# Pairwise outer products with batch norm: where the output runs of the long rows are cut

## The chip, the cores and the metric

The kernel runs on one core of a Trainium2 chip. The metric is the device time of one execution in microseconds (us). Four runs of the kernel before gave 1876.79 to 1878.18 us, with a median of 1877.02 us.

## The reference, cut to what matters

Two inputs `xi` and `xj` have the shape (1024 samples, 39 features, 16). For each of the 741 feature pairs (r, c) with c < r and each sample, the 16 x 16 outer product of `xj[r]` and `xi[c]` is taken, normalised per pair over all samples, and multiplied by a 16 x 16 weight:

```python
rows, cols = np.tril_indices(39, k=-1)                       # 741 pairs
cross  = xj[:, rows, :, None] * xi[:, cols, None, :]         # 1024 x 741 x 16 x 16
mean   = cross.mean((0, 2, 3));  var = ((cross - mean) ** 2).mean((0, 2, 3))
normed = (cross - mean) * rsqrt(var + 1e-5) * gamma + beta
out    = normed * W                                          # 776.99 MB of f32
```

The inputs are 6 MB; the output is 777 MB. "Row r" below means the r pairs (r, 0) to (r, r-1), which lie side by side in the output: r KB (r times 256 f32) of each sample.

## The kernel before, in words

The 1024 samples lie on 128 partitions with 8 samples each. The statistics come first, in about the first 40 us; they give a scale and a shift for every pair. The rest of the time is a stream of **tiles**. A tile is one row r of T = 2 samples (t = 0 and 1) on all partitions. The list `tiles` (lines 67 to 76) starts with the four tiles of row 19 (n = 0 to 3), then goes through row 20 with row 18, row 38 alone, row 37 with row 1, row 36 with row 2, and so on to row 21 with row 17, four sample pairs for each. From row 37 on, a long row and its partner row 38 - r fill together one half, a **slot**, of the buffer `y_sb`; the two slots are used in turn (`slot ^= 1`). So while one slot leaves for memory, the other is computed, and a slot can be overwritten only when its stores have landed.

For each tile the engines do this:

- `scale_xi` (line 163): GpSimd (POOL) multiplies `xi` by the scale, two tiles ahead.
- `products` (line 177): for t = 0 and then t = 1, 16 products, one for each i; ScalarE (ACT, line 147) does the first 11 or 12 of them and POOL (line 149) the rest. Each product writes all pairs of one sample. So the products of sample t wait until all earlier runs of that sample in the slot have landed.
- `finish` (line 256): the shift and the weight. VectorE (DVE) does a pair of both samples in one `scalar_tensor_tensor` (line 293), in the order of the pairs; POOL does a few pairs. In a row above `LONG` = 33 these are eight pairs before the middle (pairs 10 to 17 of row 37): ACT adds the shift (line 277) and POOL multiplies four pairs at a time (line 282). In a row up to 33 these are the last pairs (28 to 31 of row 32), shift and weight both on POOL (lines 279 and 282).
- `store` (line 205): SyncE (SP) issues the transfer of a piece of a row when its pairs are ready. All stores are issued on SP, in order, and share one queue into the core's 16 DMA engines (q1 of the profile).

`bounds` (line 247) cuts a row into pieces, and `store` into runs. A tile with n >= 8 and a row up to `WHOLE` is stored by sample: the pieces of t = 0 each by a run of its own, and t = 1 by one run of the whole row at the end. A row above `WHOLE` sends the first piece of both samples as one run, and then the last piece of each sample. A row up to `ONE` has a single piece:

| row | runs before: pair range and sample |
|---|---|
| 38 | 0:19 both; 19:38 t0; 19:38 t1 |
| 37 | 0:18 both; 18:37 t0; 18:37 t1 |
| 36 | 0:19 t0; 19:36 t0; 0:36 t1 |
| 35, 34, 33 | 0:20, 0:21, 0:22 of t0; the rest of t0; all of t1 |
| 32 | 0:23 t0; 23:32 t0; 0:32 t1 |
| 31 | 0:24 t0; 24:31 t0; 0:31 t1 |
| 30 to 20 | all of t0; all of t1 |

Rows below 19 send one run of both samples. The program order (line 525) is, for each n: `scale_xi(n + 2)`, `finish(n)`, `products(n + 1)`. The loop `for n in range(1, len(tiles))` has four long tiles to each row; with their partners between them the tiles of row 37 are n = 16, 18, 20, 22, those of row 32 are n = 56, 58, 60, 62, and those of row 31 are n = 64, 66, 68, 70. The tile that used a slot before tile n is tile n - 4 of the same kind (n = 14 for n = 16, whose row 38 has no partner, and so on).

Of the kernel before, what the change touches and what calls it, by code (L numbers as in the profile page):

```python
# [15 lines left out]

ONE, LONG, WHOLE = 30, 33, 36
FIRST_PIECES = (  # L20
    (0, 1, 3, 6, 10, 14, 19), (0, 4, 9, 14, 19), (0, 4, 11, 19), (0, 9, 19), (0, 10, 20), (0, 9, 18), (0, 10, 20), (0, 9, 18)
)
# [541 lines left out]
```

## Time and profile before

| | |
|---|---|
| median of four runs | 1877.02 us |
| the profiled execution: its time | 1878.18 us |
| the profiled execution: span from first to last instruction | 1876.5 us |
| DVE, ACT, POOL busy | 1723.7, 1645.3, 1535.5 us (92, 88, 82% of the span) |
| written to HBM | 776.99 MB, 417 GB/s over the span |
| DMA packets of the store queue (q1) | 53344, busy 98.0% of 16 engines' span |
| chain of waits: DMA, ACT, DVE | 54%, 21%, 19% of the span |

In the profile DVE, ACT, POOL and SP are the engines, a "q" behind a name means the engine's instruction sequencer (SPq issues DMAs), and L216 is line 216 of the kernel. A row of a timeline gives the start, the duration, the engine, the line, the operation, what it writes and reads, and in brackets the idle time before it and what ended that idle time. A row of DMA issues gives how many were issued in the window asked for, the KB of each, and the time from issue to landing. With the issue time from the timeline, issue plus this time is when the data has landed.

### The profile page before, as it was taken

The page shows a single profiled execution, that of the slowest core. Times are in us where ns is not written, and L with a number is a line of the kernel's source. Part 1 is how long each engine was busy: PE and PEld are TensorE (multiplying, and loading weights), DVE is VectorE, ACT ScalarE, POOL GpSimd, SP SyncE. Part 2 cuts the span into 40 slices and gives each one's busy share as a digit, 9 for nine tenths or more (in the row PEclk, how much of TensorE's full clock was granted, in tenths as well). Part 3 has the DMA queues.
Part 4 walks back from the last instruction along what each step waited for, and adds up shares of the span by engine and source line. Part 5 has one row for each costly group of instructions (what it writes and reads, how often), then busy time and mean ns, then how long its engine had stood idle before and what let it go on. Part 6 is the DMA issues. An engine that isn't in the chain of part 4 may idle for free.

```text
span 1876.5 us, 9638 instructions
## 1 busy us (share of the span) xinstructions
PE 26.0 (1%) x130; PEld 23.3 (1%) x130; DVE 1723.7 (92%) x2640; ACT 1645.3 (88%) x3416; POOL 1535.5 (82%) x1746
## 2 busy tenths in 40 slices
PE   4000000000000000000000000000000000000000
PEld 4000000000000000000000000000000000000000
DVE  8999888899999999999999999999999999999994
ACT  7999888898888899989999999998999998989892
POOL 8999877787777788888888888888888888888882
DMA  5999999999999999999999999999999999999998
GB/s 191 386 422 419 431 424 425 426 425 425 425 425 428 428 426 426 425 426 425 423 426 425 433 424 427 429 425 431 424 431 426 429 425 429 429 425 431 428 425 350
DMA packets 54714, 783.63 MB, mean 418 GB/s; under 512 B 4720, under 2 KB 6384, under 8 KB 17520
## 3 DMA queue, kind: packets, MB, share of 16 engines
q1 hardware_dynamic: 53344, 779.72, 98.0%
q10 hardware_dynamic: 1296, 3.29, 0.5%
q14 instruction: 73, 0.60, 0.1%
q8 instruction: 1, 0.02, 0.0%
HBM read 6.00 MB, written 776.99 MB: 417 GB/s over the span
## 4 chain that ended last, share of the span: by engine, by line
DMA 54%; ACT 21%; DVE 19%; issue 3%; POOL 2%; SPq 0%; ACTq 0%; DVEq 0%; PE 0%; POOLq 0%
DMA out_dram<-y_sb 54%; ACT y_sb L147 20%; DVE y_sb L293 18%; POOL y_sb L149 1%; DVE y_sb L360 1%; POOL y_sb L282 0%; ACT y_sb L230 0%; DVE y_sb L334 0%; POOL xs L169 0%; DMA xi_sb<-in_r_xi_dram 0%; POOL y_sb L279 0%; SPq L216 0%; POOL y_sb L344 0%; ACT y_sb L277 0%; DVE y_sb L192 0%
## 5 line engine op out<-in xcount | busy, mean ns | idle before, releaser
L293 DVE SCALAR_TENSOR_TENSOR y_sb<-y_sb,st_sb,w_dve 128x512 f32<-128x512 f32 (+1 forms) x2511 | 1653.1, 737 | 115.5 <-issue 101.6
L147 ACT ACTIVATE y_sb<-xs,xj_sb 128x288 f32<-128x288 f32 (+20 forms) x3194 | 1513.8, 565 | 179.8 <-DMA out_dram<-y_sb 147.3
L149 POOL TENSOR_SCALAR y_sb<-xs,xj_sb 128x480 f32<-128x480 f32 (+27 forms) x1126 | 606.9, 566 | 8.5 <-DMA out_dram<-y_sb 8.4
L282 POOL TENSOR_TENSOR y_sb<-y_sb,w_sb 128x2048 f32<-128x2048 f32 (+3 forms) x155 | 517.8, 3346 | 89.8 <-ACT y_sb L277 80.2
L169 POOL TENSOR_TENSOR xs<-xi_sb,st_sb 128x640 f32<-128x640 f32 (+33 forms) x135 | 184.3, 1365 | 198.2 <-ACT y_sb L147 194.4
L279 POOL TENSOR_SCALAR y_sb<-y_sb,st_sb 128x512 f32<-128x512 f32 x291 | 197.6, 696 | 5.1 <-ACT y_sb L147 5.1
L277 ACT ACTIVATE y_sb<-y_sb,st_sb 128x512 f32<-128x512 f32 x160 | 100.2, 708 | 4.0 <-POOL y_sb L149 2.3
L192 DVE TENSOR_TENSOR y_sb<-xs,ps 128x256 f32<-128x256 f32 (+3 forms) x32 | 24.8, 817 | 0.6
L491 PE MATMUL ps<-y_sb 39*128 39x38 f32 (+37 forms) x76 | 16.4, 397 | 2.8 <-DVE y_sb L477 2.8
L491 PEld LDWEIGHTS ps<-y_sb 39*128 39x128 f32 x76 | 16.3, 329 | 3.1 <-DVE y_sb L477 3.1
L355 ACT ACTIVATE y_sb<-y_sb 128x1248 f32<-128x1248 f32 x8 | 10.0, 1244 | 2.9 <-POOL y_sb L344 1.8
L344 POOL TENSOR_TENSOR y_sb<-xi_sb,y_sb 128x1248 f32<-128x1248 f32 x4 | 9.2, 2329 | 3.2 <-ACT y_sb L393 3.2
L360 DVE TENSOR_REDUCE y_sb<-y_sb 128x78 f32<-128x1248 f32 x8 | 11.2, 1446 | 0.4 <-ACT y_sb L355 0.4
L147 ACT ACTIVATE y_sb<-xi_sb,xj_sb 128x304 f32<-128x304 f32 x24 | 11.4, 537 | 0.0
L239 DVE TENSOR_TENSOR y_sb<-y_sb,w_dve 128x2048 f32<-128x2048 f32 (+4 forms) x6 | 10.7, 1837 | 0.1
L334 DVE TENSOR_REDUCE y_sb<-xi_sb 128x39 f32<-128x624 f32 (+1 forms) x6 | 6.1, 1013 | 3.9 <-DMA xi_sb<-in_r_xi_dram 3.9
L344 POOL TENSOR_TENSOR y_sb<-xj_sb,y_sb 128x1248 f32<-128x1248 f32 x4 | 9.2, 2330 | 0.0
L380 PE MATMUL ps<-y_sb 128*39 128x79 f32 x48 | 8.1, 340 | 16.2 <-DVE y_sb L360 16.0
L232 POOL TENSOR_SCALAR y_sb<-y_sb,st_sb 128x512 f32<-128x512 f32 x8 | 6.5, 816 | 2.1 <-ACT y_sb L147 2.1
L334 DVE TENSOR_REDUCE y_sb<-xj_sb 128x39 f32<-128x624 f32 (+1 forms) x6 | 6.1, 1015 | 0.8 <-DMA xj_sb<-in_r_xj_dram 0.8
L230 ACT ACTIVATE y_sb<-y_sb,st_sb 128x512 f32<-128x512 f32 x9 | 6.5, 803 | 0.2 <-ACT y_sb L147 0.2
L380 PEld LDWEIGHTS ps<-y_sb 128*39 128x39 f32 x48 | 5.8, 177 | 18.2 <-DVE y_sb L360 10.6
(59 smaller groups left out, 37.4 us busy)
## 6 DMA issues: line engine op xcount, KB each, us to landing
out_dram<-y_sb SPq DMA_DIRECT2D x16, 3072.0 KB, 21.9
out_dram<-y_sb SPq DMA_DIRECT2D x20, 2432.0 KB, 12.5
out_dram<-y_sb SPq DMA_DIRECT2D x10, 4608.0 KB, 15.1
out_dram<-y_sb SPq DMA_DIRECT2D x12, 3840.0 KB, 21.6
out_dram<-y_sb SPq DMA_DIRECT2D x16, 2816.0 KB, 22.4
out_dram<-y_sb SPq DMA_DIRECT2D x12, 3584.0 KB, 23.1
out_dram<-y_sb SPq DMA_DIRECT2D x12, 3328.0 KB, 24.4
out_dram<-y_sb SPq DMA_DIRECT2D x15, 2560.0 KB, 11.9
```

What stands on the lines that cost most here:

```text
L147: nc.scalar.activation(y, src, AF.Copy, scale=scale)
L149: engine.tensor_scalar(y, src, scale, 1.0, ALU.mult, ALU.mult)
L169: nc.gpsimd.tensor_tensor(xs, xi_sb[:, t0 : t0 + T, 0:r, :], s_sb[:, :, n0 : n0 + r, :].to_broadcast([P, T, r, E]), ALU.mult,)
L192: nc.vector.tensor_tensor(view(n)[:, t].rearrange("p n (i j) -> p n i j", j=E), xs[:, t].unsqueeze(2).to_broadcast([P, r, E, E]), xj_short ...
L277: nc.scalar.activation(y[:, :, c, :], y[:, :, c, :], AF.Identity, bias=t_c)
L279: nc.gpsimd.tensor_scalar(y[:, :, c, :], y[:, :, c, :], t_c, 1.0, ALU.add, ALU.mult)
L282: nc.gpsimd.tensor_tensor(y[:, :, c0:c1, :], y[:, :, c0:c1, :], w_sb.unsqueeze(1).to_broadcast([P, T, c1 - c0, EE]), ALU.mult,)
L293: stt(y[:, t : t + size, c, :], y[:, t : t + size, c, :], t_sb[:, n0 + c : n0 + c + 1], w_dve.to_broadcast([P, size, EE]), ALU.add, ALU.mult,)
L344: nc.gpsimd.tensor_tensor(devs[n % 7], sources[x][:, t0 : t0 + T], shift[:, x : x + 1, :].unsqueeze(3).to_broadcast([P, T, F, E]), ALU.sub ...
L360: nc.vector.tensor_reduce(to[:, t0 : t0 + T, F : 2 * F], devs[n % 7], AX.X, ALU.add)
L380: nc.tensor.matmul(ps_g[acc][0:F, 0 : 2 * F + 1], lhs, fb[:, t], start=t == 0, stop=t == NT - 1)
L491: nc.tensor.matmul(ps[:, :, first[r] - n0 : first[r] - n0 + r], pick[:, r, :], stq[:, :, 0:r], start=True, stop=True,)
```

## The change

Three limits are raised. Nothing else is edited.

```diff
-ONE, LONG, WHOLE = 30, 33, 36
+ONE, LONG, WHOLE = 32, 33, 37
```

`bounds` and `store` read them (lines 247 to 254 and 205 to 219), and these runs differ:

| row | runs before | runs after |
|---|---|---|
| 37 | 0:18 both; 18:37 t0; 18:37 t1 | 0:19 t0; 19:37 t0; 0:37 t1 |
| 36 | 0:19 t0; 19:36 t0; 0:36 t1 | 0:21 t0; 21:36 t0; 0:36 t1 |
| 35 | 0:20 t0; 20:35 t0; 0:35 t1 | 0:21 t0; 21:35 t0; 0:35 t1 |
| 34 | 0:21 t0; 21:34 t0; 0:34 t1 | 0:23 t0; 23:34 t0; 0:34 t1 |
| 33 | 0:22 t0; 22:33 t0; 0:33 t1 | 0:23 t0; 23:33 t0; 0:33 t1 |
| 32 | 0:23 t0; 23:32 t0; 0:32 t1 | 0:32 t0; 0:32 t1 |
| 31 | 0:24 t0; 24:31 t0; 0:31 t1 | 0:31 t0; 0:31 t1 |

The arithmetic, its order on DVE, ACT and POOL, and the order of the bytes by sample within rows 36 to 31 stay as they are. Eight transfers fewer are issued, one for each tile of rows 32 and 31.

## The prediction

> **What bounds the kernel now.** I read the page's slices first, then the chain of waits, then the single stores.
>
> ```profile
> DMA  5999999999999999999999999999999999999998
> GB/s 191 386 422 419 431 424 425 426 425 425 425 425 428 428 426 426 425 426 425 423 426 425 433 424 427 429 425 431 424 431 426 429 425 429 429 425 431 428 425 350
> q1 hardware_dynamic: 53344, 779.72, 98.0%
> ```
>
> The DMA engines are full from the second slice to the last, at about 426 GB/s whatever the row: the output's bytes set the time. A change in how runs are cut can win little here, but it can lose: a moment in which the queue is empty is added to the end. So the question is how much work the queue still holds when the next store comes. The chain of waits in rows 33 and 32:
>
> ```profile
> 727.62 18.88 DMA out_dram<-y_sb
> 746.50 0.02 issue
> ...
> 750.16 19.90 DMA out_dram<-y_sb
> 770.06 0.02 issue
> ```
>
> This is a loop: the landing of sample 1 (746.50, 770.06) frees a slot, ACT goes on, and later that slot's stores are issued. The timeline gives its length:
>
> ```profile
> 770.14 21.18 ACT L147 ACTIVATE y_sb<-xs,xj_sb 128x512 f32<-128x512 f32 x48 [2.38 <-DMA out_dram<-y_sb]
> 777.69 18.52 DVE L293 SCALAR_TENSOR_TENSOR y_sb<-y_sb,st_sb,w_dve 128x512 f32<-128x512 f32 x28 [1.75 <-issue]
> ```
>
> The first 12 of the 48 products (sample 1 of tile 60) end at 777.6, and DVE's 28 pairs at 0.66 us end at 796.21. SP issues then. From landing to the end of the row it is 796.28 - 770.06 = 26.22 us, in all four tiles of row 32. The stores themselves, issues from the timeline and KB with time to landing from the DMA issues, for row 5's last store and the second piece of row 32 (tile 56), and two stores early in the run:
>
> ```profile
> 729.90 0.38 SPq L216 DMA_DIRECT2D out_dram<-y_sb  x1
> 749.73 0.33 SPq L216 DMA_DIRECT2D out_dram<-y_sb  x1
> ...
> 61.68 0.33 SPq L216 DMA_DIRECT2D out_dram<-y_sb  x1
> 64.43 0.38 SPq L216 DMA_DIRECT2D out_dram<-y_sb  x1
> ```
>
> ```profile
> out_dram<-y_sb SPq DMA_DIRECT2D x1, 1280.0 KB, 19.7
> out_dram<-y_sb SPq DMA_DIRECT2D x1, 1152.0 KB, 9.8
> ...
> out_dram<-y_sb SPq DMA_DIRECT2D x1, 640.0 KB, 3.4
> out_dram<-y_sb SPq DMA_DIRECT2D x1, 1024.0 KB, 4.0
> ```
>
> I call the landing of the last store issued so far, less the time of the next issue, the **lead**. When row 32's first piece is issued, at 746.51, the queue holds work until 729.90 + 19.7 = 749.6, a lead of 3.1 us. No lead behind the start-up is under 1.4 us (row 38: 240.10 + 16.7 against an issue at 255.36). How much lead is needed shows at 64.43: the queue ended at 61.68 + 3.4 = 65.1 (lead 0.6); 1024 KB take 2.4 us (two stores of 2432 KB, issued at 214.76 and 215.14 and landing after 13.3 and 18.7 us, lie 5.7 us apart: 434 GB/s); but it landed at 68.4, 1.6 us after its issue and 2.4 more. The store at 68.92 found an empty queue and gives 1.6 us too. So a **dry spell** is 1.6 us less the lead, if that is positive.
>
> **The change part by part.** *Row 32.* DVE's order stays, so the single run of sample 0 goes out when now the second piece does, 3.2 us later than the first piece. The leads at that time, from the partner's last store (row 5 or 6) and the second piece's issue:
>
> - tile 56: 749.6 - 749.73 = -0.1, a dry spell of 1.7 us
> - tile 58: 753.09 + 20.6 - 772.72 = 1.0; plus 1.7
> - tile 60: 776.09 + 20.6 - 796.28 = 0.4
> - tile 62: 799.65 + 20.4 - 819.26 = 0.8
>
> Now the loop counts. The dry spell ahead of tile 56 delays the queue's end by 1.7, but tile 58 comes 26.22 us after tile 54's landing, which is not delayed: its lead is 2.7, no loss. Tile 60 comes after tile 56's landing, 1.7 later like the queue: lead 0.4 as before, dry for 1.2. Tile 62 has 0.8 + 1.2 = 2.0: none. Row 32 costs 1.7 + 1.2 = 2.9 us. Behind the waiting store SP holds only sample 1's store and the partner's; sample 1's is issued 0.4 us later in either case, and ACT waits for its landing, which moves with the queue.
>
> *Row 31.* The same sum with 7 KB partners: 822.63 + 21.3 - 841.67 = 2.3, then 1.7, 2.6 and 1.6 us. Nothing, but with no reserve. Row 30, which already leaves this way, has 3.2 us at 934.54.
>
> *Row 37.* The first run now carries one sample: 2432 KB or 5.7 us in place of 4608 KB, while the next store comes 7.5 us after it. When it is issued is set by POOL, not by DVE:
>
> ```profile
> 290.49 9.97 DVE L293 SCALAR_TENSOR_TENSOR y_sb<-y_sb,st_sb,w_dve 128x512 f32<-128x512 f32 x15 [3.36 <-ACT y_sb L147]
> 293.19 9.01 POOL L282 TENSOR_TENSOR y_sb<-y_sb,w_sb 128x2048 f32<-128x2048 f32 x2 [5.67 <-ACT y_sb L277]
> ```
>
> POOL ends at 302.20 and the store is issued at 302.24; DVE's eleventh pair (pair 18, the added one) is done at 290.49 + 11 x 0.66 = 297.8, so it costs nothing. Tile 16: the queue ends at 263.85 + 17.1 = 281.0, with the short run at 286.7; the second run comes at 285.50: lead 1.2, dry for 0.4. Tile 18: 287.21 + 17.2 + 0.4 + 5.7 = 310.5 against 309.70: 0.8, dry for 0.8. Tiles 20 and 22 gain: sample 0 now lands ahead of sample 1's bytes, some 5 us sooner, so ACT need not wait for it as it does for 3.25 us ahead of 321.17. For tile 20 ACT can begin when its shifts end, 295.5, and is through sample 0's 11 products at 303.0; sample 1's landing, 285.88 + 18.1 + 0.4 = 304.4, is late next, against a start at 305.3 now: 0.9 us of 2.3 is left. With that and the 1.2 us by which the queue has moved, the second stores of tiles 20 and 22 have over 2.5 us of lead. Row 37 costs 1.2 us.
>
> *Rows 36 to 33.* First pieces longer by one or two pairs. In rows 36 to 34 POOL's multiply sets the first issue as above, and a longer piece only adds lead to the second. In row 33 the issue is 0.66 us later; its smallest lead, 2.9 us at 676.33, covers that and without it would become a dry spell of up to 0.66. Nothing.
>
> *Eight stores fewer.* SP idles between stores, so its 0.33 us each are hidden. On the DMA side, tile 58's two pieces land at 780.6 and 783.4 after a queue end of 773.7, 9.7 us, and its sample 1 in one run of the same bytes at 793.05, 9.6 us: at most 0.1 us a tile, 0.8 us in all; taken as 0, since the two agree to the rounding. [...]
>
> The sum is 2.9 + 1.2 = 4.1, taken as 4.0 against the rounding of the leads. On the profiled execution's own time, 1878.18, that is 1882.2; that execution lies 1.2 above the median of 1877.02, so the median becomes 1881.0 us (+0.21%). Bounds: if a store needed no lead at all, only tile 56's 0.1 us would remain; if no dry spell helped the next tile, 1.7 + 0.6 + 1.2 + 0.8 in row 32 and 0.4 + 1.2 in row 37 give 5.9.
>
> **The rivals.**
>
> 1. *Every tile pays.* The alternation fails, because the products that were late delay both slots. Price 5.9: 1882.9 us. For it: ACT runs 48 products without a pause between two landings and DVE is at 92%. Against: ACT still has 1.8 to 2.4 us of waiting in each loop.
> 2. *The transfers stay hidden.* The queue's landing is that of its slowest engine; if the others, which are further on, give way while it catches up, a dry spell costs little: 1877 to 1879 us. For it: the last rows of the trace (below) show most engines through long before the slowest. Against: the store at 64.43 paid in full.
> 3. *Faster: the engines are made level.* At the end one or two engines work alone:
>
> ```profile
> 1867.00:1869.00 2.00, 0.00 (x0) 0.00 (x0) 0.00 (x0) 0.00 (x0) 0.00 (x0) 1.00 0.24 104
> 1869.00:1875.50 6.50, 0.00 (x0) 0.00 (x0) 0.00 (x0) 0.00 (x0) 0.00 (x0) 1.00 0.11 46
> ```
>
> The columns after the engines are clock, DMA share and GB/s. In the last 8.5 us a share of 0.24 and then 0.11 of 16 engines is busy. A dry queue lets the late engine catch up; if it stayed level, up to 8.5 us would go, 1881.0 - 8.5 = 1872.5. It decides from 4.0 us of gain on, the dry spells' price. Against: the share is over 0.95 until 1866, so what delays that engine goes on for 1000 us after row 32.
>
> **How the numbers follow.** The sum above has 0.5, rival 1 0.2, rival 2 0.25, rival 3 0.05. The range leaves out rival 3, half of rival 2 and the upper edge: 1878.3 to 1883.2; the likeliest case alone has 1879.8 to 1882.0. A measurement of this kernel can tell about 0.2% (3.75 us) from no change, so slower begins at 1880.8, just under the forecast: slower has a bit over half of the first case and all of rival 1, and some of the upper tail, 0.51; same 0.46, from the rest of the first case and rival 2; faster 0.03, the far part of rival 3.
>
> **What would show it.** Right: in row 32 the DMA share falls for 1 to 3 us ahead of tiles 56 and 60 (near 750 and 797) and not ahead of 58 and 62; near 286 and 310 it dips less; ACT starts tile 20's and 22's products straight after its eight shifts; row 31 is full. The landing to issue time stays 26.22 us. Wrong: dips ahead of all four tiles or in row 31 (rival 1, or a need of more than 1.6 us), none at all (rival 2), or a last window whose DMA share stays high to the end (rival 3).

## The result, and the profile after

The changed kernel takes 1880.39 us (median of 32 runs, 1879.88 to 1880.84), against 1876.97 us for the kernel before (52 runs). The ratio is 1.0018, with a 95% interval of [1.0013, 1.0023]: 3.4 us slower. The profiled execution took 1880.45 us. Its span is 1878.7 us, only 2.2 us above that of before, because the profiled execution of before lay 1.2 us above its median: its first store was issued at 36.79 us, here at 35.67. Stages are therefore compared below by their lengths and not by the clock.

The slices and the store queue of the kernel after:

```profile
GB/s 200 387 418 423 430 425 412 426 425 428 427 427 425 425 425 405 413 434 425 424 427 430 425 431 426 430 426 428 428 429 426 430 424 429 428 426 431 428 425 355
q1 hardware_dynamic: 51680, 779.72, 97.9%
```

The queue moves the same bytes in 1664 packets fewer. Three slices stand out with 412, 405 and 413 GB/s: the seventh (282 to 329 us, row 37) and the sixteenth and seventeenth (705 to 798 us, the end of row 33 and row 32). No other slice has lost as much. Next, short windows of the kernel after; the last two columns are the share of the 16 DMA engines and GB/s. They lie around the stores of tiles 56, 58, 60 and 62 (row 32), of tiles 16 and 18 (row 37), and of tiles 64 and 66 (row 31). A share above 1 comes from packets that are counted whole where they begin (from 760 to 761 us of the kernel before, two packets of q1 that take 17.4% of the 16 engines' time, so 1.4 us each on average, stand in one slice of 25 ns each). For the same reason half a microsecond of shift can move the share of so short a window by up to 0.3 (here 0.64 from 797.0 to 801.0 us and 0.93 from 797.5 to 801.5 us), so the windows show where a dip lies, and the leads and landings below measure it.

```profile
748.00:752.00 4.00, 0.00 (x0) 0.00 (x0) 4.00 (x7) 4.00 (x7) 2.83 (x5) 1.00 0.67 283
773.00:777.00 4.00, 0.00 (x0) 0.00 (x0) 2.84 (x5) 4.00 (x7) 1.24 (x2) 1.00 1.11 470
797.00:801.00 4.00, 0.00 (x0) 0.00 (x0) 3.90 (x6) 4.00 (x8) 1.92 (x3) 1.00 0.64 270
821.00:825.00 4.00, 0.00 (x0) 0.00 (x0) 2.89 (x5) 4.00 (x8) 0.81 (x2) 1.00 1.13 476
284.00:288.00 4.00, 0.00 (x0) 0.00 (x0) 1.94 (x5) 4.00 (x7) 2.42 (x2) 1.00 0.73 300
308.00:312.00 4.00, 0.00 (x0) 0.00 (x0) 3.22 (x7) 3.91 (x7) 2.61 (x2) 1.00 0.75 310
844.00:848.00 4.00, 0.00 (x0) 0.00 (x0) 3.93 (x6) 4.00 (x8) 1.96 (x3) 1.00 1.16 491
867.00:871.00 4.00, 0.00 (x0) 0.00 (x0) 4.00 (x7) 4.00 (x8) 2.80 (x5) 1.00 0.98 410
```

The same places in the kernel before, tiles 56, 60, 16 and 18:

```profile
747.00:751.00 4.00, 0.00 (x0) 0.00 (x0) 4.00 (x8) 4.00 (x8) 3.98 (x6) 1.00 1.04 437
794.00:798.00 4.00, 0.00 (x0) 0.00 (x0) 4.00 (x7) 4.00 (x7) 3.52 (x6) 1.00 1.13 481
285.00:289.00 4.00, 0.00 (x0) 0.00 (x0) 2.06 (x5) 4.00 (x7) 2.52 (x2) 1.00 1.04 442
309.00:313.00 4.00, 0.00 (x0) 0.00 (x0) 2.36 (x7) 3.91 (x7) 2.74 (x2) 1.00 1.04 442
```

ACT is busy through all four dips (3.9 to 4.0 of 4 us), and DVE is nearly as busy as before or busier; what has gaps are the DMA engines, at every second tile of row 32 and in the first two tiles of row 37. The stores behind that, in the timeline and in the DMA issues of the kernel after: the partner's last store (row 5) and tile 56's single run of sample 0, then the same for tile 60 (row 6), and row 37's second runs of tiles 16 and 18.

```profile
730.04 0.38 SPq L216 DMA_DIRECT2D out_dram<-y_sb  x1
749.66 0.33 SPq L216 DMA_DIRECT2D out_dram<-y_sb  x1
775.98 0.38 SPq L216 DMA_DIRECT2D out_dram<-y_sb  x1
797.75 0.33 SPq L216 DMA_DIRECT2D out_dram<-y_sb  x1
284.37 0.33 SPq L216 DMA_DIRECT2D out_dram<-y_sb  x1
308.56 0.33 SPq L216 DMA_DIRECT2D out_dram<-y_sb  x1
```

```profile
out_dram<-y_sb SPq DMA_DIRECT2D x1, 1280.0 KB, 19.4
out_dram<-y_sb SPq DMA_DIRECT2D x1, 4096.0 KB, 12.1
out_dram<-y_sb SPq DMA_DIRECT2D x1, 1536.0 KB, 22.1
out_dram<-y_sb SPq DMA_DIRECT2D x1, 4096.0 KB, 11.2
out_dram<-y_sb SPq DMA_DIRECT2D x1, 2304.0 KB, 6.9
out_dram<-y_sb SPq DMA_DIRECT2D x1, 2304.0 KB, 7.0
```

Tile 56 comes when the queue is empty (730.04 + 19.4 = 749.4 against 749.66). Tile 60 comes with 0.3 us of lead (798.1 against 797.75). Its 4096 KB need 9.7 us (tile 58's run of sample 1 has as many bytes and lands at 794.45, 9.7 us after that of sample 0, 772.69 + 12.1 = 784.8), so from issue to landing 1.5 us go to the start. (Tile 56's 12.1 us hold about 1 us more than that; the part on row 32 below comes back to it.) Tile 16's second run has 276.91 + 8.7 - 284.37 = 1.2 us of lead and tile 18's 301.11 + 8.5 - 308.56 = 1.0; their 2304 KB need 5.4 us at 434 GB/s and land 6.9 and 7.0 us after the issue, again 1.5 and 1.6 us.

Measured from the landing of the store before it to the landing of its last partner store, the stage of row 32 takes 94.3 us before (749.6 to 843.9) and 96.7 us after (749.4 to 846.1): 2.4 us more. The stage of row 37 takes 93.9 us (281.0 to 374.9) and 95.2 us (279.8 to 375.0): 1.3 us more. Together that is 3.7 us. Rows 34 and 33 are 0.2 us shorter each, and the other stages add up to 0.2 us more. The chain of waits of the kernel after shows the same loop as before, with longer DMA pieces in front:

```profile
750.09 21.37 DMA out_dram<-y_sb
771.46 0.02 issue
...
773.12 21.32 DMA out_dram<-y_sb
794.45 0.02 issue
...
798.19 20.47 DMA out_dram<-y_sb
```

The store of tile 60 is issued 797.75 - 771.46 = 26.29 us after the landing that frees its slot, 26.22 us before the change: the computing has not become slower.

### The profile page after: what moved, and what is told of

The parts are those of the page before. It is cut to its first block, busy times and chain, and to the rows that moved or that the text cites. A ratio compares the mean times of both kernels' runs of the same rounds, so it can differ in the third digit from the quotient of the medians.

```text
span 1878.7 us, 9610 instructions
## 1 busy us (share of the span) xinstructions
PE 26.0 (1%) x130; PEld 23.3 (1%) x130; DVE 1723.7 (92%) x2640; ACT 1645.8 (88%) x3416; POOL 1535.5 (82%) x1746
## 4 chain that ended last, share of the span: by engine, by line
DMA 39%; ACT 12%; DVE 7%; issue 1%; SPq 0%; ACTq 0%; DVEq 0%
DMA out_dram<-y_sb 39%; ACT y_sb L147 12%; DVE y_sb L293 7%; SPq L216 0%; ACTq L147 0%; DVEq L559 0%; DVEq L293 0%
## 5 line engine op out<-in xcount | busy, mean ns | idle before, releaser
L380 PEld LDWEIGHTS ps<-y_sb 128*39 128x39 f32 x48 | 5.8, 177 | 17.1 <-DVE y_sb L360 10.6
```

The costliest lines, as they stand in the source:

```text
L380: nc.tensor.matmul(ps_g[acc][0:F, 0 : 2 * F + 1], lhs, fb[:, t], start=t == 0, stop=t == NT - 1)
```

## The experiments

The theory: the whole loss is the time in which the store queue is empty. A store issued with less than about 1.6 us of lead leaves it empty for the rest, and a dry spell gives lead to the next tile, so that tiles pay alternately. The rivals: every tile pays; the cost lies in the whole runs or in the longer first pieces themselves; a dry spell is hidden; the levelling of the DMA engines pays for it. All medians below have runs of the kernel before on the same chip beside them (1876.84 to 1876.95 us). The limits are `ONE, LONG, WHOLE`.

### Rows 32 and 31 alone

```diff
-ONE, LONG, WHOLE = 30, 33, 36
+ONE, LONG, WHOLE = 32, 33, 36
```

> Rows 32 and 31 in one run per sample, rows 37 to 33 cut as before. Theory (a dry spell is 1.6 us less the lead, and one dry spell gives lead to the next tile): dry for 1.7 us ahead of tile 56 and 1.2 us ahead of tile 60, nothing at tiles 58 and 62 and in row 31: 2.4 to 2.9 us slower than before. Rival 'every tile pays': 4.3 us slower, dips ahead of all four tiles. Rival 'hidden': within 1 us of before. Were the loss in row 37 or in the longer first pieces of rows 36 to 33, this kernel would be as fast as before.

Measured: 1879.43 us (11 runs, 1879.20 to 1879.88) against 1876.89, ratio 1.0013 [1.0003, 1.0022]: 2.5 us slower. The leads from its trace are -0.2, 2.5, 0.3 and 1.7 us for tiles 56, 58, 60 and 62. In the trace row 32's stage is 2.4 us longer than before and row 37's is unchanged. That is what the theory gives with alternation; the leads at tiles 58 and 62 leave no dry spell there, and four of them would have cost 4.3 us.

### Row 37 alone, with the longer pieces

```diff
-ONE, LONG, WHOLE = 30, 33, 36
+ONE, LONG, WHOLE = 30, 33, 37
```

> Row 37 by sample, longer first pieces in rows 36 to 31 (row 32 is cut at 25, row 31 at 25), rows 32 and 31 still in pieces. Theory: dry for about 0.3 us ahead of the second run of tile 16 and 0.5 us in tile 18, no dip elsewhere (row 32's smallest lead is 3.1 - 2 x 0.66 = 1.8 us): 0.8 to 1.3 us slower than before. Together with the kernel that changes rows 32 and 31 alone this should make up the 3.4 us of the change. Rival 'hidden': within 0.3 us. If the longer first pieces mattered, rows 36 to 33 would lose bytes per time too.

Measured: 1878.16 us (11 runs, 1877.72 to 1878.51), ratio 1.0006 [0.9997, 1.0015]: 1.3 us slower, though the interval of the ratio holds 1. The windows of this kernel around the two stores:

```profile
284.00:288.00 4.00, 0.00 (x0) 0.00 (x0) 1.57 (x4) 4.00 (x7) 2.01 (x1) 0.50 0.90 374
308.00:312.00 4.00, 0.00 (x0) 0.00 (x0) 3.23 (x8) 3.91 (x7) 2.21 (x2) 0.50 0.91 378
```

The share is 0.9 in both, and that alone says little: against the stores these two windows begin 0.4 us later than those of the kernel after, and a window begun 0.4 us sooner, 283.6 to 287.6, has 0.73. The firmer evidence is in the stores: the second runs of tiles 16 and 18 have leads of 1.2 and 1.0 us, and row 37's stage is 1.3 us longer than in the trace of before, as in the kernel after. The two parts add up to 3.8 us, the whole change is 3.4; the difference is within the intervals.

### Row 31 alone

```diff
-ONE, LONG, WHOLE = 30, 33, 36
+ONE, LONG, WHOLE = 31, 33, 36
```

> Row 31 alone in one run per sample, all else as before. Theory: its leads of 2.3, 1.7, 2.6 and 1.6 us are enough: 0 within 0.3 us of before. If a store needs 2.0 us of lead, two tiles of row 31 are dry for 0.3 and 0.1 us: 0.4 us slower. [...]

Measured: 1877.07 us (11 runs) against 1876.89, ratio 1.0000 [0.9992, 1.0009]. Row 31's leads were 2.2, 1.7, 2.4 and 1.8 us, and that is enough: no loss that can be measured, and no gain from four transfers fewer.

### One row further: row 33 too

```diff
-ONE, LONG, WHOLE = 30, 33, 36
+ONE, LONG, WHOLE = 33, 33, 36
```

> Rows 33, 32 and 31 in one run per sample, rows 37 to 34 as before: one row further into the loss. The leads at row 33's whole run are -0.9, -1.6, -0.1 and -0.6 us. Theory, each dry spell added to the next tile's lead: 2.5, 0.7, 0.95, 1.3 in row 33 and 0.4, 0.2, 1.0, 0 in row 32: 7.0 us slower than before. Rival 'every tile pays': 2.5 + 3.2 + 1.7 + 2.2 and 4.3 in row 32: 13.9 us slower. Rival 'hidden': within 2 us.

Measured: 1884.28 us (5 runs, 1883.96 to 1884.35), ratio 1.0038 [1.0025, 1.0050]: 7.4 us slower. This is the run that parts the theory (7.0) from "every tile pays" (13.9). Windows of this kernel around the stores of tiles 48, 50, 52, 54 (row 33) and 56 (row 32):

```profile
655.00:659.00 4.00, 0.00 (x0) 0.00 (x0) 3.50 (x6) 4.00 (x8) 1.47 (x3) 1.00 0.64 270
679.00:683.00 4.00, 0.00 (x0) 0.00 (x0) 3.15 (x5) 4.00 (x7) 1.36 (x3) 1.00 0.92 384
704.00:708.00 4.00, 0.00 (x0) 0.00 (x0) 3.14 (x5) 4.00 (x8) 1.11 (x2) 1.00 0.65 274
728.00:732.00 4.00, 0.00 (x0) 0.00 (x0) 3.69 (x6) 4.00 (x8) 1.56 (x3) 1.00 0.84 352
752.00:756.00 4.00, 0.00 (x0) 0.00 (x0) 4.00 (x7) 4.00 (x8) 2.15 (x4) 1.00 0.95 397
```

Tile 48 finds the queue empty since 1.0 us; its 4224 KB (10.0 us) are issued at 656.01 and land 11.5 us later, 1.5 us for the start and 2.5 us dry in all. Tile 50, whose lead by the trace of before would have been -1.6, has 1.0 here: the dry spell ahead of tile 48 came back as lead. So it does for tile 56 (1.4 in place of -0.1), which the change itself lets run dry. By the stages of the trace row 33 takes 6.1 us more than before and row 32 1.0 us more, where the expectation had 5.5 and 1.6: the sum fits better than its parts.

### Row 37 by sample, with a longer first piece

```diff
-ONE, LONG, WHOLE = 30, 33, 36
+ONE, LONG, WHOLE = 30, 33, 37
...
+        if r == 37:
+            return 0, 25, r
```

> Limits 30, 33, 37 as in the run with row 37 alone (1.27 us slower than before), but row 37's first piece has 25 pairs in place of 19: 7.5 us of transfer for the 7.5 us until the next store. Theory: the second run's lead stays near the first's, 2.2 to 2.9 us, so no dry spell in row 37: within 0.3 us of before, and not faster, since the earlier landing of sample 0 is worth nothing while the queue is full. Rival 'row 37 by sample costs by itself (one run of 37 KB, another order of landing)': still about 1.3 us slower.

Measured: 1876.57 us (11 runs, 1876.13 to 1876.91) against 1876.95, ratio 0.9998 [0.9989, 1.0007]. The 1.3 us are gone, with the same single run of 37 KB for sample 1: the slowest run here is faster than the fastest of the run with row 37 alone (1877.72), and row 37's stage, 1.3 us longer than before there, is 0.3 us shorter than before here. The leads of the second runs are 3.0, 2.0, 4.3 and 4.7 us. So neither the single run nor the order of the samples costs anything that can be measured; the too short first piece did. The median is the lowest of all kernels here, 0.4 us below that of before, but the interval doesn't tell the two apart.

### Whole runs in row 32, issued sooner: six pairs on GpSimd, and five

```diff
-ONE, LONG, WHOLE = 30, 33, 36
+ONE, LONG, WHOLE = 32, 33, 36
...
             share = int(r * POOL_SHARE + 0.5) if r > SHORT else 0
+            if r == 32:
+                share = 6
```

> Rows 32 and 31 in one run per sample (2.54 us slower than before), and in row 32 GpSimd finishes six pairs in place of four, so VectorE has 26 and row 32's store is issued 2 x 0.66 = 1.3 us sooner after the landing. The runs stay whole. Theory: leads of 1.2, 2.3, 1.7 and 2.1 us, one dry spell of 0.4 us at tile 56: 0.1 to 0.6 us slower than before. Rival 'whole runs cost by themselves': still 2.5 us slower. GpSimd gets about 3.6 us more to do in each of the four tiles and might come last; then some of the loss stays.

Measured with six: 1877.25 us (11 runs) against 1876.95, ratio 1.0002 [0.9992, 1.0011]: 0.3 us slower. The windows of this kernel around the stores of tiles 56, 58 and 60:

```profile
746.00:750.00 4.00, 0.00 (x0) 0.00 (x0) 4.00 (x7) 4.00 (x7) 3.92 (x6) 1.00 0.76 319
769.00:773.00 4.00, 0.00 (x0) 0.00 (x0) 4.00 (x7) 3.84 (x7) 3.92 (x6) 1.00 1.16 484
793.00:797.00 4.00, 0.00 (x0) 0.00 (x0) 4.00 (x7) 4.00 (x8) 3.92 (x6) 1.00 0.99 416
```

One small dip is left, ahead of tile 56, whose lead was 1.2 us; tile 60's was 1.5. GpSimd is now busy nearly all of the time (3.92 of 4 us). Its multiply did not come last, but VectorE had to wait for its products, so tile 62's store came 25.6 us after the landing that frees its slot, in place of the 24.9 that were meant, and had a lead of 1.3 us and not 2.1. Row 31's first store then had 1.3 us too. By the stages of the trace row 32 takes 0.1 us more than before and row 31 0.5 us more. With five pairs (`share = 5`):

> Rows 32 and 31 in one run per sample, GpSimd finishes five pairs of row 32 (four: 2.54 us slower than before; six: 0.30 us). The store comes 0.66 us sooner than with four. Theory: leads of 0.5, 1.7, 1.1 and 1.4 us, dry for 1.1 us at tile 56 and 0.5 us at tile 60: 1.2 to 1.6 us slower than before, between the two.

Measured: 1878.35 us (11 runs, 1878.07 to 1878.71) against 1876.84, ratio 1.0008 [0.9999, 1.0016]: 1.5 us slower, between the two; the interval just holds 1, but no run of it is as fast as the slowest of before (1877.44). Its leads at tiles 56 and 60 were 0.4 and 0.8 us. The same runs in the queue cost 2.5, 1.5 or 0.3 us; what differs is who finishes one or two pairs of row 32, and so when the store is issued.

### The change with its lead given back

```diff
-ONE, LONG, WHOLE = 30, 33, 36
+ONE, LONG, WHOLE = 32, 33, 37
...
+        if r == 37:
+            return 0, 25, r
...
             share = int(r * POOL_SHARE + 0.5) if r > SHORT else 0
+            if r == 32:
+                share = 6
```

> The kernel of the change with all its whole runs, except that row 37's first piece has 25 pairs and GpSimd finishes six pairs of row 32, so that both places with a dry spell get lead. Theory: the dry spells are the whole loss, so it is 3.0 to 3.6 us faster than the change and within 0.5 us of before. Were part of the loss in the longer first pieces, in the whole runs or in row 31, that part would stay.

Measured: median 1877.01 us (11 runs, ten of them 1876.78 to 1877.23 and one 1881.43) against 1876.84, ratio 1.0003 [0.9994, 1.0012]: 0.2 us from before, 3.4 us less than the change. All whole runs and longer pieces of the change are in it, with row 37's first piece longer still. What sets it apart from the change is the lead of its stores.

### The end of the run: a cut by partitions, twice

The last 8.5 us of the kernel before show a tenth to a quarter of the DMA engines at work. Two kernels tried to keep the late engines out of the last store; they differ from the kernel before only in how its partitions are cut. The second has `(0, 105, 126, 128)`.

```diff
+            cuts = (0, 120, 127, 128) if n == len(tiles) - 1 else (0, P)
+            for a, z in zip(cuts, cuts[1:]):
-            nc.sync.dma_start(
-                out_v[:, t0 + t : t0 + t + step, (n0 + c0) * EE : (n0 + c1) * EE],
+                nc.sync.dma_start(
+                    out_v[a:z, t0 + t : t0 + t + step, (n0 + c0) * EE : (n0 + c1) * EE],
```

> The kernel before, but the last store of all (row 17, 4.5 MB) is cut into partitions 0 to 119, 120 to 126 and 127. If the cut keeps the last of the DMA engines out of this store, and that engine is the one that ends 2.7 us behind the next and 8.5 us behind the rest, the end comes up to 2.7 us sooner. If the late engine is another one, the time stays within 0.5 us of before or grows by up to 2 us, from the two added stores. The dry spells have no part in this.

> The kernel before, the last store cut into partitions 0 to 104, 105 to 125 and 126 to 127. If the first part spreads over 15 engines and the second over 7, the late engine has nothing of this store and the second latest less of it: up to 4.0 us sooner than before. If the late engine is not among those left out: up to 3 us slower, since the lower engines get more to move.

Measured: 1887.06 us (ratio 1.0053 [1.0041, 1.0066]) and 1886.64 us (1.0051 [1.0038, 1.0063]), 10 us slower each; both expectations missed. The windows of the first, ahead of the cut store and in it:

```profile
1840.00:1850.00 10.00, 0.00 (x0) 0.00 (x0) 8.54 (x13) 0.00 (x0) 2.36 (x2) 1.00 1.03 439
1856.00:1864.00 8.00, 0.00 (x0) 0.00 (x0) 0.00 (x0) 0.00 (x0) 0.00 (x0) 1.00 0.94 248
```

The engines are nearly as busy as before and move little more than half. The slowness isn't the cut store's alone: the store ahead of it, sample 1 of row 21 (2688 KB), is not cut, and it lands 34.3 us after its issue here and 25.6 us in the kernel before. Whether one engine could be spared at the end stays open.

## Why the prediction was right

The median was forecast at 1881.0 us and came to 1880.39; the forecast of slower by 4.0 us is 3.4 us in the measurement, within the range, and just under the 0.2% that was taken for the limit of what can be told. That limit was too wide for this kernel: the runs of before and after don't overlap, and 3.4 us is clear of no change.

*What bounds the kernel*: right. The queue at about 426 GB/s sets the time, and the change adds to it by empty moments.

*Row 32, 2.9 us*: right in place and pattern (tile 56 and tile 60 dry, 58 and 62 not), a little too large: 2.5 us in the run with rows 32 and 31 alone. The lead of tile 60 was 0.3 us and its start took 1.5 us, as worked out to a tenth. From the landing of the store ahead to that of sample 1, tile 56 takes 1.6 us more than before, tile 60 1.0 us more and tile 62 0.2 us less: the two dry tiles cost a little less than their terms of 1.7 and 1.2 us, and a tile without a dry spell gave 0.2 us back. Tile 56's first run landed 12.3 us after the store ahead, 2.7 us more than its 9.7 us of bytes, of which 1.7 us are the dry spell. The other 1 us is not new: in the kernel before sample 1's run of the same tile had it (749.73 + 9.8 = 759.5 to 770.06, 10.6 us), and in the kernel after that run is free of it (749.66 + 12.1 = 761.8 to 771.46, 9.7 us). In both traces a packet of the instruction queue (q14) begins inside the delayed run, at 760.4 us before and at 759.4 after. Whether that is the cause no run tested.

*The alternation*: shown by row 33's run, 7.4 us against 7.0 and 13.9. Rival 1 is out.

*Row 31, nothing, with no reserve*: right, 0.2 us, inside its interval.

*Row 37, 1.2 us*: right in place, and 1.3 us alone, but that the sum fits so well is in part luck. By the leads of 1.2 and 1.0 us against the 1.5 to 1.6 us needed, the two dry spells were nearer to 0.3 and 0.5 us than to 0.4 and 0.8; the term of tile 18 was too large, because its lead had been worked out as 0.8. The other 0.5 us is spread over the stage in small parts, and no run says what they are. Tiles 20 and 22 did as said: ACT took up the products where its shifts ended, and the wait came back at sample 1. The second stores of the two tiles had leads of 3.2 and 3.1 us. ACT's timeline in the kernel after, for the products of tile 20:

```profile
289.36 5.01 ACT L277 ACTIVATE y_sb<-y_sb,st_sb 128x512 f32<-128x512 f32 x8
294.28 7.57 ACT L147 ACTIVATE y_sb<-xs,xj_sb 128x592 f32<-128x592 f32 x11
303.24 7.58 ACT L147 ACTIVATE y_sb<-xs,xj_sb 128x592 f32<-128x592 f32 x11 [1.40 <-DMA out_dram<-y_sb]
```

The shifts end at 294.37, the first 11 products start with no gap, and 1.40 us of waiting stands ahead of the second 11. The first piece of 25 pairs keeps this early start, and its kernel is 0.4 us faster than before, which the interval doesn't tell from nothing.

*Rows 36 to 33, and eight transfers fewer, nothing*: right, as far as can be measured; the kernel with its lead given back has both and lies 0.2 us from before. Row 31's four transfers fewer, alone, changed nothing that can be measured (1877.07 us against 1876.89). In these runs a start cost shows where a store finds the queue empty or nearly so: 1.5 to 1.6 us at tiles 60, 16 and 18 after the change (leads of 0.3, 1.2 and 1.0 us), and 1.5 us at tile 48 of row 33's run (-1.0 us).

*Rival 2*, hidden: out, since the loss moves with the lead (2.5, 1.5, 0.3 us). *Rival 3*, levelling: no gain from it is seen. The end of the kernel after:

```profile
1869.50:1871.50 2.00, 0.00 (x0) 0.00 (x0) 0.00 (x0) 0.00 (x0) 0.00 (x0) 1.00 0.25 104
1871.50:1877.80 6.30, 0.00 (x0) 0.00 (x0) 0.00 (x0) 0.00 (x0) 0.00 (x0) 1.00 0.10 44
```

Here too the last 8.3 us are a quarter and then a tenth of the engines. Whether the dry spells didn't level the engines, or they did and the late one fell behind again in the 1000 us that follow, these views don't show.

## What to carry to other kernels

Where a queue of stores sets the time, read for each store how much work the queue still holds when it is issued. Here, joining transfers was free as long as that lead stayed above the start of a transfer (1.5 to 1.6 us), brought no gain that could be measured while the queue was full, and cost the missing lead where it didn't. And before four tiles' losses are added up, look whether the loop that issues the stores is released by the same queue: here a dry spell gave its time back as lead to the next tile, and the loss was about half of the sum (7.4 us against 13.9).

## What the runs showed that was not expected

With the last store cut at 120 partitions the DMA engines moved 248 GB/s at a share of 0.94, where ahead of it they moved 439 GB/s at a share of 1.03, and the uncut store just ahead of it in the queue slowed down too. No run here shows why the engines moved less, or separates one cause from another. Each of the two cuts cost 10 us, and the cut store, 4352 KB, needs 10.3 us at 434 GB/s.
